# Loading and converting the first chunk of the masked weight by quarters, with fewer zero products ahead of it

## The chip, the cores and the metric

The kernel runs on one core of a Trainium2 chip. Its time is the device time of one execution in microseconds (us); the time before is the median of 3 runs, 395.11 us (395.07 to 395.71). A core has a tensor engine for matrix products (PE, with its weight loads shown apart as PEld), a vector engine (DVE), a scalar engine (ACT), a general engine (POOL) and a queue engine that mostly issues transfers (SP). Transfers (DMAs) run on 16 DMA engines beside them. Products are summed in PSUM, of which the kernel uses 8 banks; everything else lies in SBUF.

## The reference, cut to what matters

The input x has 8 batches of 256 tokens by 1024 features. Two residual layers follow each other. The first adds to x a dense layer and a difference whose weight is the sign that an integer mask stands for, scaled by a number per batch:

```python
def _L0_cond_ref(hidden_states, W, b, coeff, mask):
    output = jnp.einsum('bsi,oi->bso', hidden_states, W) + b
    sign = (2 * mask - 1).astype(hidden_states.dtype)
    diff = jnp.einsum('bsi,bio->bso', hidden_states, sign)
    return output + diff * coeff[:, None, None]

x = x + _L0_cond_ref(x, L0_cond_W, L0_cond_b, condB_coeff, mask)
x = x + _L1_cond_ref(x, itok, L1_cond_W, L1_cond_b, L1_cond_lora_As, L1_cond_lora_Bs)
```

The second adds a dense layer with weight W1, one bias, and a rank-16 adapter chosen per batch. All is in float32. The kernel folds the first layer into one weight per batch, W0 + coeff * (2 * mask - 1), plus the identity for the residual.

## The kernel before, in words

Batch 0 is computed directly and is what the change touches. Its weight is built in eight chunks `c` of 128 input features; each chunk has two parts `i` of 512 output columns. For each part, SP issues a load of 128 x 512 mask integers and a load of 128 x 512 numbers of W0 (256 KB each; the loop at the call of `first_loads`, recorded at L400). ACT converts the mask to float as 2 * coeff * mask - coeff (`convert`, L488), DVE adds W0 in place (`add`, recorded at L387), and PE multiplies each 128 x 128 block of the sum with the 128 x 256 block of x (L570). The last step has eight output blocks for each chunk, four for each part, accumulated in four banks. A float32 product appears in the trace as two MATMUL records.

Two small numbers per batch, `two_c` and `neg_c` (L445), hold 2 * coeff and -coeff on all partitions. They come from a tiny product of PE (L435) on the loaded coefficients, and the first conversion needs them. Before and behind this product PE multiplies zeros into a bank that nobody reads (`idle`, L422): 256 and 128 columns before it, 256, 256 and 128 columns behind it. The real products of batch 0 follow in PE's queue directly behind the last zeros.

`parts(c)` says in what pieces a chunk is converted and summed. In chunk 0 part 0 goes in two pieces of 256 columns, so that the first two output blocks can start once the first piece is there; part 1 and all other chunks go in pieces of 512 columns. The loads are never smaller than 512 columns.

After batch 0 come batches 1 to 3 by a seven-product scheme (`seven`, products at L761), then the second layer for four batches at once (`second_layer`, L1089, L1144, L1223, L1254), and then the same for batches 4 to 7. In batch 1 the weight is made in another way: ACT writes W0 - coeff (`shifted`, L500), and DVE adds 2 * coeff * mask to it (L645). DVE also makes the sums and differences of weights and tokens that the scheme needs, and adds the identity to W0 in SBUF, one 128 x 128 block per chunk (`identity`, L387).

The order of every engine's queue is fixed when the kernel is built, by a planner (`Plan`): each step has an estimated duration, PE's steps follow each other without a gap from a start that the code sets (`plan.pe = 5.2` for batch 0), and the other engines' steps are placed by the due times that follow from PE's. So a change of that start shifts due times and can swap steps on DVE, ACT, POOL and SP anywhere in the program.

In the second group of four, `left_again` loads again from DRAM the sums of the second layer's weights that the first group saved; for the name in `HALVES` two of them are loaded by two DMAs each, of 128 KB.

Of the kernel before, what the change touches and what calls it, by code (L numbers as in the profile page):

```python
# [9 lines left out]
I32 = mybir.dt.int32  # L10
# [3 lines left out]
P = 128  # L14
OH = 512
CG = 2
OQ = 256
# [6 lines left out]
A22_AT = 40.0  # L24
INNER_MOVED, INNER_AT = ({}, {o: ("t1", "t2", "t3", "t4") for o in ("S3", "A22")}), 24.0
SAVED = {(o, n) for o in ("A11", "S1", "S4") for n in ("a11", "s1")}
HALVES = ("A11",)
EARLIEST = 35.0
SHIFTED, MASKED = 5.2, 1.8
LEAF, SLACK = 30.0, 1.5  # L30
ALONE = 8.0
# [273 lines left out]
def kernel(  # L305
# [17 lines left out]
    NG, _, _, T = x0T.shape  # L323
# [41 lines left out]
    def small(name, a, b):  # L365
        return Buf(name, "S", (a, b))
# [12 lines left out]
    plan = Plan(2.9)  # L379
# [14 lines left out]
    def dma(engine, o, x, nbytes, due=None, ahead=None, slack=0.0):  # L394
        busy = {"SP": 0.37, "ACT": 0.36, "POOL": 0.53}[engine]
        reads = [x] if isinstance(x, Ref) else []
        writes = [o] if isinstance(o, Ref) else []

        def emit():
            ENGINE[engine].dma_start(  # L400
                o.ap() if isinstance(o, Ref) else o, x.ap() if isinstance(x, Ref) else x
            )

        return plan.task(
            engine, busy, plan.LATENCY[engine] + slack, emit, reads, writes, due, ahead, nbytes
        )

    def pe(n, busy, emit, reads, writes):
        return plan.task("PE", busy, 0.17, emit, reads, writes)
# [9 lines left out]
    def idle(*columns):  # L419
        def emit():  # L420
            for n in columns:
                nc.tensor.matmul(  # L422
                    idle_ps.t[:, 0, :n], lhsT=zeros[:, :P], rhs=zeros[:, :n], start=True, stop=True
                )

        pe(1, sum(columns) / 290, emit, (), (idle_ps((0,)),))
# [11 lines left out]
        (h_sb(h_rows), lb_pad((0, 1))),  # L438
        (c_ps((0,)),),
    )  # L440
    idle(T, T, T // 2)
    plan.pe = 5.2
    for o, f in ((two_c, 2.0), (neg_c, -1.0)):
        dve(
            lambda o=o, f=f: nc.vector.tensor_scalar_mul(o.t, c_ps.t[:, 0, :B], f),  # L445
# [6 lines left out]
    def x0_ref(p, c=None):  # L452
        return x0[p](ALL if c is None else (c,), (lambda t: t) if c is None else (lambda t: t[:, c]))
# [4 lines left out]
    def part(a, i):  # L458
        flat = a.rearrange("p i f -> (p i f)")
        return flat.rearrange("(i p f) -> i p f", i=2, p=P)[i]  # L460

    def parts(c):
        every = slice(0, OH)
        if c == 0:
            return [(0, slice(0, OQ)), (0, slice(OQ, OH)), (1, every)]
        return [(0, every), (1, every)]

    def halves(o):
        return tuple(q for q in range(2) if o.start < (q + 1) * OQ and o.stop > q * OQ)
# [38 lines left out]
    def w_part(c, i, o):  # L508
        return w_b0[c](tuple((i, q) for q in halves(o)), lambda t: t[:, i, o])

    def w0_part(c, i, o):
        return w0_sb(
            tuple((c, i, q) for q in halves(o)),
            lambda t: t[:, c, :].rearrange("p (h o) -> p h o", h=2)[:, i, o],
        )

    def first_loads(*load):
        k = dma(*load)
        k.rank = 1.0 + 0.001 * k.n

    every = slice(0, OH)
    for c in range(NC):
        for i in range(2):
            w = w_part(c, i, every)
            m = w.buf(w.keys, lambda t, f=w.index: f(t).bitcast(I32))
            first_loads("SP", m, part(mask[0, c], i), P * OH * 4)
            first_loads("SP", w0_part(c, i, every), part(w0T[c], i), P * OH * 4)
            if c < CG and i == 0:
                first_loads(("ACT", "SP")[c], x0_ref(0, c), part(x0T[0], c), P * T * 4)
            elif c % CG == 0 and i == 0:  # L530
                first_loads("SP", x0_ref(c // CG), x0T[c // CG], P * CG * T * 4)
# [19 lines left out]
    for c in range(NC):  # L551
        h, q = divmod(c * P, OH)
        for i, o in parts(c):
            w = w_part(c, i, o)
            m = w.buf(w.keys, lambda t, f=w.index: f(t).bitcast(I32))
            n = o.stop - o.start
            convert(w, m, 0, n)
            if c >= 1 and i == h and o.start <= q < o.stop:
                d = w_b0[c](((h, q // OQ),), lambda t, h=h, q=q: t[:, h, q : q + P])
                add(d, d, ident((0,)), P)  # L560
            add(w, w, w0_part(c, i, o), n)
    for c in range(NC):
        for i, o in parts(c):
            ots = [i * TPH + j for j in range(o.start // P, o.stop // P)]
            w = w_part(c, i, o)
# [297 lines left out]

    SOON = EARLIEST
    A_OF = {"a11": (0, 0), "a12": (0, 1), "a22": (1, 1)}
# [53 lines left out]
    def left_again(name, pairs=()):  # L919
# [21 lines left out]
        for n in saved:  # L941
            t = small(f"ls_{name}_{n}", 4, P)
            step = 2 if name in HALVES else 4
            for i in range(0, 4, step):
# [731 lines left out]
```

## Time and profile before

| what | value |
|---|---|
| median of 3 runs | 395.11 us |
| the profiled execution | 395.16 us |
| its span, first to last instruction | 393.5 us |
| PE busy in the span | 389.7 us (99%), 2920 records |
| DVE busy | 352.2 us (90%), 596 instructions |
| ACT busy | 169.8 us (43%), 314 instructions |
| DMA from the hardware queue of SP | 68.76 MB |
| zero products, ahead of and behind the tiny product | 10 records, from 0.90 to 5.46 us |
| products of batch 0 | 128 records, from 5.46 us, 29.03 us of the chain |

Columns of a timeline row: start in us from the span's start, length in us, engine, line, operation, output<-input tiles, shapes, number of instructions merged, and in brackets the idle time ahead of the row and what ended it. PE's records overlap, since matmuls are pipelined: the work rate is read from the distance between starts, not from a record's length. The profiled execution lasted 1.7 us longer than its span, and 0.05 us longer than the median.

### The profile page before, as it was taken

The page shows a single profiled execution, that of the slowest core. Times are in us where ns is not written, and L with a number is a line of the kernel's source. Part 1 is how long each engine was busy: PE and PEld are TensorE (multiplying, and loading weights), DVE is VectorE, ACT ScalarE, POOL GpSimd, SP SyncE. Part 2 cuts the span into 40 slices and gives each one's busy share as a digit, 9 for nine tenths or more (in the row PEclk, how much of TensorE's full clock was granted, in tenths as well). Part 3 has the DMA queues.
Part 4 walks back from the last instruction along what each step waited for, and adds up shares of the span by engine and source line. Part 5 has one row for each costly group of instructions (what it writes and reads, how often), then busy time and mean ns, then how long its engine had stood idle before and what let it go on. Part 6 is the DMA issues. An engine that isn't in the chain of part 4 may idle for free.

```text
span 393.5 us, 7725 instructions
## 1 busy us (share of the span) xinstructions
PE 389.7 (99%) x2920; PEld 363.8 (92%) x2920; DVE 352.2 (90%) x596; ACT 169.8 (43%) x314; POOL 84.2 (21%) x140
## 2 busy tenths in 40 slices
PE   9999999999999999999999999999999999999997
PEld 7889999999978898988899999999999789999896
DVE  3569999999897799989999989999996999999886
ACT  5469677516245221315615647373222563431210
POOL 1000202234734264252250330000000131241000
PEclk9999999999999999999999999999999999999999
DMA  8999999994899969989999998503702999995804
GB/s 290 389 389 410 404 300 389 318 346 156 198 269 290 270 239 368 417 247 317 348 347 338 291 260 304 191 1 108 242 0 61 262 238 265 324 255 101 263 31 185
DMA packets 39382, 102.50 MB, mean 261 GB/s; under 512 B 5170, under 2 KB 6322, under 8 KB 39346
## 3 DMA queue, kind: packets, MB, share of 16 engines
q1 hardware_dynamic: 27216, 68.76, 49.0%
q0 software_dynamic: 11840, 33.05, 32.5%
q8 instruction: 23, 0.38, 0.4%
q10 hardware_dynamic: 290, 0.20, 0.2%
q14 instruction: 13, 0.11, 0.1%
HBM read 65.82 MB, written 21.50 MB: 222 GB/s over the span
## 4 chain that ended last, share of the span: by engine, by line
PE 99%; DVE 0%; issue 0%
PE bank L761 44%; PE bank L1089 31%; PE bank L1144 11%; PE bank L570 7%; PE bank L1254 2%; PE bank L1223 2%; PE bank L422 1%; PE bank L1444 0%; PE bank L435 0%; DVE big L387 0%
## 5 line engine op out<-in xcount | busy, mean ns | idle before, releaser
L387 DVE TENSOR_TENSOR big<-big,big 128x1024 f32<-128x1024 f32 (+2 forms) x106 | 106.1, 1019 | 0.4 <-PE bank L761 0.4
L761 PE MATMUL bank<-small,big 128*128 128x128 f32 x896 | 104.6, 275 | 0.0
L761 PEld LDWEIGHTS bank<-small,big 128*128 128x128 f32 x896 | 102.3, 192 | 0.0
L387 DVE TENSOR_TENSOR big<-bank,big 128x512 f32<-128x512 f32 (+2 forms) x115 | 75.5, 678 | 15.0 <-PE bank L1089 8.2
L488 ACT ACTIVATE big<-big,neg_c,two_c 128x1024 f32<-128x1024 int32 (+2 forms) x65 | 71.1, 1123 | 19.4 <-DMA big<-mask 19.3
L761 PE MATMUL bank<-big,big 128*128 128x128 f32 x672 | 78.3, 275 | 0.0
L761 PEld LDWEIGHTS bank<-big,big 128*128 128x128 f32 x672 | 76.8, 192 | 0.1
L387 DVE TENSOR_TENSOR big<-big,w 128x1024 f32<-128x1024 f32 (+2 forms) x55 | 56.5, 1048 | 6.3 <-ACT big L488 3.4
L672 ACT ACTIVATE big<-bank,b 128x128 f32<-128x128 f32 x112 | 33.3, 367 | 52.7 <-PE bank L761 47.0
L391 ACT COPY bank<-bank 128x128 f32<-128x128 f32 (+1 forms) x42 | 14.4, 357 | 89.6 <-PE bank L1144 48.3
L1089 PE MATMUL bank<-small,small 128*128 128x256 f32 x168 | 40.2, 379 | 0.0
L1089 PEld LDWEIGHTS bank<-small,small 128*128 128x128 f32 x168 | 31.4, 190 | 3.9
L391 ACT COPY big<-bank 128x512 f32<-128x512 f32 x32 | 17.7, 594 | 36.0 <-PE bank L1254 17.4
L1089 PE MATMUL bank<-big,small 128*128 128x256 f32 x120 | 30.5, 381 | 0.0
L570 PE MATMUL bank<-small,big 128*128 128x256 f32 x128 | 29.2, 393 | 0.0
L570 PEld LDWEIGHTS bank<-small,big 128*128 128x128 f32 x128 | 25.4, 199 | 3.6
L477 POOL DMA_DIRECT2D big<-w x10 | 12.5, 1254 | 71.9 <-DMA big<-mask 56.5
L1089 PEld LDWEIGHTS bank<-big,small 128*128 128x128 f32 x120 | 21.4, 191 | 2.5 <-DVE big L387 0.4
L477 POOL DMA_DIRECT2D big<-big x14 | 12.3, 931 | 46.6 <-ACT big L991 36.1
L1089 PE MATMUL bank<-big,big 128*128 128x256 f32 x88 | 21.1, 383 | 0.0
L387 DVE TENSOR_TENSOR small<-big,small 128x512 f32<-128x512 f32 (+1 forms) x41 | 21.1, 522 | 0.0
L1089 PEld LDWEIGHTS bank<-big,big 128*128 128x128 f32 x88 | 16.5, 190 | 3.2 <-issue 0.4
(106 smaller groups left out, 468.6 us busy)
## 6 DMA issues: line engine op xcount, KB each, us to landing
big<-mask SPq DMA_DIRECT2D x56, 512.0 KB, 9.1
big<-xT SPq DMA_DIRECT2D x14, 512.0 KB, 8.6
big<-big POOLq DMA_DIRECT2D x14, 512.0 KB, 9.0
big<-w POOLq DMA_DIRECT2D x10, 512.0 KB, 10.3
big<-mask SPq DMA_DIRECT2D x16, 256.0 KB, 5.4
w<-w0T SPq DMA_DIRECT2D x16, 256.0 KB, 5.4
big<-w1T SPq DMA_DIRECT2D x8, 512.0 KB, 14.5
leaf_S_s<-small POOLq DMA_DIRECT2D x16, 256.0 KB, 7.6
```

Of the source, the lines that this page charges most:

```text
L387: return dve(lambda: f(o.ap(), x.ap(), y.ap()), n, (x, y), (o,), due, ahead)
L391: "ACT", n / 1200 + 0.06, 0.11, lambda: nc.scalar.copy(o.ap(), x.ap()), (x,), (o,), due
L422: nc.tensor.matmul(idle_ps.t[:, 0, :n], lhsT=zeros[:, :P], rhs=zeros[:, :n], start=True, stop=True)
L477: lambda: nc.gpsimd.dma_start(o.ap(), z.ap(), accum_op=ALU.add),
L488: lambda: nc.scalar.activation(o.ap(), x.ap(), AF.Identity, bias=neg_c.t[:, b : b + 1], scale=two_c.t[:, b : b + 1]),
L570: nc.tensor.matmul(dense[ot // 2].t[:, ot % 2, :], lhsT=w_b0[c].t[:, h, j * P : (j + 1) * P], rhs=x0[c // CG].t[:, c % CG, :], start=c == ...
L672: lambda o=o, p=p, bias=bias: nc.scalar.activation(o.ap(), p.ap(), AF.Identity, bias=bias.ap()),
L761: nc.tensor.matmul(ps[:, j, :], lhsT=l[:, c, j * P : (j + 1) * P], rhs=m[:, 2 * a + c, :], start=first and a == 0 and c == 0 and j == 0, s ...
L1089: nc.tensor.matmul(ps.t[:, j, :], lhsT=lt[:, c, j * P : (j + 1) * P], rhs=rt[:, c, :], start=start and c == 0 and j == 0, stop=False, skip ...
L1144: lambda: nc.tensor.matmul(o.ap(), lhsT=l.ap(), rhs=r.ap(), start=start, stop=False, skip_group_check=True),
L1223: nc.tensor.matmul(ph.t[i * S : i * S + R, 0, :], lhsT=la.t[:, i, c, :], rhs=y[GB * group + i, c // TPH].t[:, c % TPH, :], start=c == 0, s ...
L1254: nc.tensor.matmul(ps[b].t[:, j, :], lhsT=lb_pad.t[rows, o : o + P], rhs=h_sb.t[rows, :], start=j == 0, stop=j == 1, skip_group_check=True,)
```

## The change

- The load of part 0 of chunk 0 is issued as four DMAs of 128 x 256 (128 KB each: mask, W0, mask, W0) in place of two of 128 x 512. SP so has 4 issues where it had 2, and every later load is two places further back in its queue.
- Part 1 of chunk 0 is converted and summed in two pieces of 256 columns in place of one of 512. Its loads stay whole.
- Behind the tiny product PE multiplies 256 and 128 columns of zeros in place of 256, 256 and 128.
- The planner's start of batch 0's products is 4.75 in place of 5.2.
- `HALVES` is empty: in the second group the two saved sums of A11 are loaded by one DMA each (256 KB) in place of two (128 KB).

The order of PE's real products is unchanged. On the other engines the planner swaps some neighbours. The ones near the change: on DVE one addition of the identity to W0 (128 x 128) goes from ahead of the first three L645 steps of batch 1 to behind them; on ACT one L500 step of batch 1 goes ahead of the last conversion of batch 0. Later: on DVE a few sums of batches 1 to 3 and of the second layer swap places with a neighbour, on ACT some reads of banks swap with conversions, on POOL four stores of the second layer's sums change places, and on SP one mask load of the second group goes behind the loads of the saved sums.

```diff
-HALVES = ("A11",)
+HALVES = ()
+IDLE, FIRST = (256, 128), 4.75
+PARTS = 4
...
-    idle(T, T, T // 2)
-    plan.pe = 5.2
+    idle(*IDLE)
+    plan.pe = FIRST
...
     def parts(c):
         every = slice(0, OH)
         if c == 0:
-            return [(0, slice(0, OQ)), (0, slice(OQ, OH)), (1, every)]
+            first = [slice(0, OQ), slice(OQ, OH)]
+            return [(0, o) for o in first] + [(1, o) for o in (first if PARTS == 4 else [every])]
         return [(0, every), (1, every)]
...
     for c in range(NC):
         for i in range(2):
-            w = w_part(c, i, every)
-            m = w.buf(w.keys, lambda t, f=w.index: f(t).bitcast(I32))
-            first_loads("SP", m, part(mask[0, c], i), P * OH * 4)
-            first_loads("SP", w0_part(c, i, every), part(w0T[c], i), P * OH * 4)
+            for o in ((slice(0, OQ), slice(OQ, OH)) if c == i == 0 else (every,)):
+                n = P * (o.stop - o.start) * 4
+                wo = w_part(c, i, o)
+                m = wo.buf(wo.keys, lambda t, f=wo.index: f(t).bitcast(I32))
+                first_loads("SP", m, part(mask[0, c], i)[:, o], n)
+                first_loads("SP", w0_part(c, i, o), part(w0T[c], i)[:, o], n)
```

## The prediction

> **What bounds the kernel now.** I read the chain of waits first, then PE's timeline of the first microseconds, then the record lengths of batch 0's products, then the other engines around the first product, and last DVE's timeline, to see what an earlier PE would run into.
>
> ```profile
> PE 99%; DVE 0%; issue 0%
> PE bank L761 44%; PE bank L1089 31%; PE bank L1144 11%; PE bank L570 7%; PE bank L1254 2%; PE bank L1223 2%; PE bank L422 1%; PE bank L1444 0%; PE bank L435 0%; DVE big L387 0%
> ```
>
> The whole span is PE's queue from 0.90 us on. So only two things shorten it: fewer records on PE, or records that run faster. Anything else helps only if it ends a wait of PE, and PE has nearly none: the starts from 8.4 us on follow each other at 0.216 us (256 columns) or 0.112 us (128), and all that exceeds this, at changes of shape, is 2.1 us in 382.
>
> ```profile
> 0.90 1.62 PE L422 MATMUL bank<-const-float32-0.0 128*128 128x256 f32 x4 [0.90 <-PEq L1665]
> 2.45 0.79 PE L435 MATMUL bank<-lb,h 1*128 1x128 f32 x2
> 3.17 2.50 PE L422 MATMUL bank<-const-float32-0.0 128*128 128x256 f32 x6
> 5.46 3.77 PE L570 MATMUL bank<-small,big 128*128 128x256 f32 x10
> ```
>
> The six records of zeros fill 3.17 to 5.46 us; the change takes two of 256 columns out. How much time that is depends on the clock, which the lengths of batch 0's records show, up to 8.5 us and behind 8.6 us (count, then least, median and greatest length in ns):
>
> ```profile
> L570 PE MATMUL bank<-small,big x8: 381/634/635, 5.5 to 8.4; 128*128 128x256 f32 x8
> ```
> ```profile
> L570 PE MATMUL bank<-small,big x121: 379/379/381, 8.4 to 34.3; 128*128 128x256 f32 x121
> ```
>
> Until about 8.4 us a record lasts 634 ns and starts come 0.427 us apart; behind it 379 ns and 0.216 us. PE runs at half speed first, zeros included, and at full speed from 8.38 us to the end. So a microsecond gained before 8.38 us is worth only half a microsecond at the end, if the moment of the switch stays.
>
> ```profile
> 0.86 0.38 SPq L400 DMA_DIRECT2D big<-mask  x1
> ...
> 1.30 0.42 SPq L400 DMA_DIRECT2D w<-w0T  x1
> 1.42 0.36 ACTq L400 DMA_DIRECT2D small<-x0T  x1
> ...
> 3.36 0.15 DVE L445 TENSOR_SCALAR neg_c<-bank 128x8 f32<-128x8 f32 x1
> ...
> 3.75 1.09 ACT L488 ACTIVATE big<-big,neg_c,two_c 128x256 f32<-128x256 int32 x2 [0.44 <-DMA big<-mask]
> ...
> 4.76 0.76 DVE L387 TENSOR_TENSOR big<-big,w 128x256 f32<-128x256 f32 x2 [1.24 <-DMA w<-w0T]
> ```
>
> The first sum waits for the W0 load and ends at 5.18 us; PE reaches its first real product at 5.46 us, 0.28 us later. So taking zeros out alone would gain little: the sum has to come earlier too.
>
> **The zeros.** Six records begin at 3.17, 3.76, 4.19, 4.61, 5.04 and 5.25 us, the first with 0.16 us of start-up. Without two of 0.427 us they end at 4.61 us. If PE went straight on, two records of batch 0 would move into the half-speed time, which saves two full-speed records: 2 x 0.216 = 0.43 us. That is the most this part can give.
>
> **The first sum.** `neg_c` is done at 3.52 us; nothing of the change moves that. The mask's half load now carries 8 packets of 1 KB per DMA engine in place of 8 of 2 KB; near the start of the trace the former last 46 ns, the latter 84. The whole load lands at 3.66 us, the half about 8 x 38 = 0.3 us sooner, so ACT now waits for `neg_c`. It starts at about 3.59; the first conversion of 256 columns lasted 0.60: 4.19. The W0 half lands before that: today W0 ends at 4.63 behind 8 mask packets and beside x, and per engine 8 x 38 ns are saved in each of the two loads, 0.6 us: 4.03. x itself landed at 4.81; its 8 packets share the engines with lighter loads, so about 4.2. DVE starts 0.04 behind ACT (as at 6.25 behind 6.21) and lasts 0.43: 4.66. PE starts 0.07 later (the least such distance in the trace), at 4.73, and pays the start-up of 0.16 again, because it stood still from 4.61. Its second record then stands where a steady flow begun at 4.89 would have it, 0.57 us before today's 5.46. That is 0.57 / 0.427 = 1.34 records, worth 1.34 x 0.216 = **0.29 us** at the end. Bounds: 0.43 from above (no stop); from below, if the W0 half landed no sooner than today's whole, PE would start at 5.16 + 0.16 and gain 0.07.
>
> **Two more issues on SP.** An issue lasts 0.38 to 0.43 us, so each later load is issued 0.8 us later. The DMA engines don't run dry: the first packets ran 1.02 us behind their issue, so the load now fifth (issued near 2.7) can run from 3.7, while the four halves and x keep each engine busy with 40 packets of 46 ns from 2.47 to 4.31. What remains is the packets' price: 32 of 46 ns in place of 16 of 84 is +0.13 us for all loads behind, since the engines are full (near 390 GB/s) up to about 45 us. In batch 0 each sum ends 1.65 to 1.74 us before its product from the second part on: 0.13 later and 0.29 earlier leave 1.2. No stall.
>
> **Part 1 in quarters.** Two conversions cost 1.09 us (today's pair at 3.75) where one costs 0.81, two sums 0.76 where one costs 0.69. PE wants the first quarter at 4.89 + 8 x 0.427 = 8.3 us. The load lands near 5.5; conversion 0.6 and sum 0.43 make 6.6. Hidden by 1.6 us, and it buys nothing; uncovered, the whole would cost at most 0.35.
>
> **Swaps near the change.** The L500 step that goes ahead of the last conversion on ACT (1.13 us) delays it by up to 0.45; its sum ends at 30.07 and its product starts at 32.81, so 1.9 us stay. What counts is on DVE:
>
> ```profile
> 30.10 0.29 DVE L387 TENSOR_TENSOR w<-w,ident 128x128 f32<-128x128 f32 x1
> 30.31 1.28 DVE L645 SCALAR_TENSOR_TENSOR big<-big,two_c,big 128x1024 f32<-128x1024 int32 x1
> 31.51 0.69 DVE L746 TENSOR_TENSOR small<-big 128x512 f32<-128x512 f32 x1
> 32.86 2.57 DVE L645 SCALAR_TENSOR_TENSOR big<-big,two_c,big 128x1024 f32<-128x1024 int32 x2 [0.66 <-DMA big<-mask]
> ```
> ```profile
> 33.00:65.00 32.00, 32.00 (x281) 31.80 (x281) 31.97 (x31) 23.56 (x39) 4.75 (x4) 1.00 1.04 375
> ```
>
> The second line (window; sum; PE, PEld, DVE, ACT, POOL busy) shows DVE full: from the mask wait at 32.86 it stands still nowhere until 106 us. In that stretch all delays add. The addition of the identity at 30.10 takes 0.21 us of time in which DVE waits anyway; the change puts it behind 32.86, where it costs 0.21. With the load's 0.13 DVE is 0.34 us late. The tightest sum of the stretch is the second of the pair at 61.84, which ends at 64.20; its product starts at 64.91. PE wants it at 64.91 - 0.29 - 0.07 = 64.55, DVE has it at 64.20 + 0.34 = 64.54. That is even, and I take **0.05 us** as lost there (0 to 0.29). The next tightest have 1.03 us (45.3) and 1.38 us (81.0).
>
> **The rest.** Behind 106 us DVE waits for PE's banks again and again, so it moves with PE; the swaps there exchange neighbours of 0.7 to 1.2 us where no bank read goes later. The loads of `HALVES` are issued at 243.7 to 249.2 us, land within 4.8 us and serve products at 297.9: 45 us of cover; one mask load goes two issues back, 0.8 us. POOL's stores serve loads a hundred microseconds later. The tail behind PE's last record (390.3 to 393.5) keeps its steps. Price 0; if a cover failed, a step's length, 0.7 to 1.2.
>
> **The sum**: 395.16 - 0.29 + 0.05 = 394.92 against the profiled execution, which stands 0.05 above the median; so 394.9.
>
> **A rule of the Trainium skill beside this.** "TensorE: Matmul & The Clock Gate", Part 1: The HAM clock gate, says that PE starts at half clock and is released after a busy window of about 3.4 us, windows that run freely and don't start with the kernel. The trace agrees on half speed. By the page a stop inside the window that would have released the clock costs a whole window, and it speaks against a change that makes PE wait: by it, as an estimate, the switch comes 3.4 us later and the time is about 396.6; if the stop falls outside, it is 394.9 as above.
>
> **Rivals.**
> - *The clock comes later* (slower than before). The change makes PE stop at 4.61, where today it runs on. For: today PE ran without a stop from 3.17 to the switch at 8.38, 5.21 us; if that time counts from the last stop, the switch comes at 4.73 + 5.21 = 9.94, 1.56 us later, half of it lost: 394.9 + 0.78 = 395.7. If the 7.48 us from the first record (0.90) count anew from there, it comes at 12.2, and the time is 396.8. Against: the stop is 0.12 us, and the stops at 2.31 and 3.04 today did not keep the switch from coming. It is over 0.2% slower if the switch comes behind 10.4 us.
> - *The clock comes earlier*, with real products: 5.46 to 8.38 is 2.92 us; 4.73 + 2.92 = 7.65, 0.73 us of half speed less, 0.36 gained: 394.5. Against: zeros keep PE just as busy.
> - *DVE eats it.* The 64.9 us product waits the whole 0.29 or somewhat more: 395.1 to 395.3. It is slower by 0.2% only if DVE is 1.4 us late there, for which I find 0.34.
> - *The start doesn't move*: the W0 half or x lands as today, gain 0.07: 395.1.
>
> **How the numbers follow.** 0.2% is 0.8 us, about what a measurement of this kernel can tell from no change. Chances: forecast (394.7 to 395.0) 0.55; later clock 0.19, of which 0.13 past 0.2%; earlier clock 0.13, of which 0.09 past 0.2%, where it comes earlier still; DVE and the unmoved start 0.13. So faster 0.10, same 0.76, slower 0.14. The range, 394.3 to 396.0, runs from the earlier clock to between the two later ones; what it leaves out is about 0.2.
>
> **What would show it.** PE's zeros end at 4.6 us and the first L570 record starts at 4.7 to 4.9, behind a stop of about 0.1; the first conversion starts near 3.6, the first sum near 4.25. L570 records change from 634 to 379 ns at about 8.4 us; a change at 9.9 or 11.8 means the later clock. The first L761 record stands at 34.25 in place of 34.54. DVE has no gap from 33 to 106 us; a wait of PE on DVE near 64.6 is the second rival. I am wrong if the switch moves, or if PE waits anywhere behind 35 us for more than a few tenths.

## The result and the profile after

The changed kernel takes 396.39 us (median of 10 runs, 395.74 to 397.57) against 395.05 us of the kernel before (median of 10 runs beside it, 394.69 to 395.71). The ratio is 1.0036, with a 95% interval of 1.0025 to 1.0046: it is slower by 1.3 us. The prediction said 394.9, within 0.2% of before.

The profiled execution after the change took 396.84 us with a span of 395.2 us, 1.7 us more than the span before. Its page has this chain of waits (share of the span by engine, then by line; L766 is the former L761, L1094 the former L1089, L575 the former L570):

```profile
PE 82%; DMA 8%; DVE 6%; issue 2%; SPq 1%; DVEq 0%
PE bank L766 37%; PE bank L1094 30%; PE bank L1149 11%; DMA big<-mask 4%; DVE big L389 4%; DMA w<-w0T 3%; PE bank L1259 2%; PE bank L1228 2%; DVE big L650 2%; SPq L402 1%; PE bank L1449 0%; DVE small L751 0%; DVE w L389 0%; DVEq L650 0%
```

Before, 99% of the chain was PE's own queue. Now 15% of it are loads of masks and W0, SP's issues of them, and DVE's work on them. The end no longer goes back through PE to the start: it goes back through DVE and the first loads.

The timeline of the first microseconds shows what came as foreseen and what did not:

```profile
2.71 0.43 SPq L402 DMA_DIRECT2D big<-mask  x1
...
3.17 1.65 PE L424 MATMUL bank<-const-float32-0.0 128*128 128x256 f32 x4
...
3.56 0.60 ACT L491 ACTIVATE big<-big,neg_c,two_c 128x256 f32<-128x256 int32 x1 [0.26 <-DVE neg_c L447]
...
4.19 0.43 DVE L389 TENSOR_TENSOR big<-big,w 128x256 f32<-128x256 f32 x1 [0.67 <-ACT big L491]
4.57 0.60 ACT L491 ACTIVATE big<-big,neg_c,two_c 128x256 f32<-128x256 int32 x1 [0.41 <-DMA big<-mask]
...
4.67 5.15 PE L575 MATMUL bank<-small,big 128*128 128x256 f32 x15
...
5.56 0.42 DVE L389 TENSOR_TENSOR big<-big,w 128x256 f32<-128x256 f32 x1 [0.95 <-DMA w<-w0T]
...
6.76 1.09 ACT L491 ACTIVATE big<-big,neg_c,two_c 128x256 f32<-128x256 int32 x2 [1.59 <-DMA big<-mask]
```

The first conversion (3.56), the first sum (4.19) and the first product (4.67) stand where the prediction put them, the product 0.80 us sooner than before. But then the loads are late: the second W0 half holds the second sum until 5.56, and mask part 1, issued at 2.71 in place of 1.77, holds the conversion of part 1 until 6.76. By its last packet that mask landed at 6.73 us; before the change it landed at 5.38.

Here are the DMA engines in windows of 2 us (window; sum; PE, PEld, DVE, ACT, POOL busy with counts; PE clock; busy share of the DMA engines; GB/s). Before the change:

```profile
2.00:4.00 2.00, 2.00 (x7) 1.46 (x6) 0.24 (x2) 1.55 (x3) 0.31 (x1) 1.00 0.89 298
4.00:6.00 2.00, 2.00 (x7) 1.64 (x7) 0.96 (x3) 1.44 (x3) 0.00 (x0) 1.00 1.06 385
6.00:8.00 2.00, 2.00 (x6) 1.58 (x5) 1.01 (x3) 1.03 (x2) 0.00 (x0) 1.00 1.06 389
```

After it:

```profile
2.00:4.00 2.00, 2.00 (x7) 1.46 (x6) 0.24 (x2) 1.73 (x3) 0.31 (x1) 1.00 0.91 265
4.00:6.00 2.00, 2.00 (x6) 1.59 (x6) 0.86 (x3) 0.75 (x2) 0.00 (x0) 1.00 0.93 228
6.00:8.00 2.00, 2.00 (x6) 1.39 (x6) 0.69 (x3) 1.09 (x2) 0.00 (x0) 1.00 1.04 372
```

Between 4 and 6 us the engines count as busy 93% of the time but move 228 GB/s in place of 385. Their packets show where the time went: the usual one of 1 KB takes 46 ns and the usual one of 2 KB 84 ns, but between 3.5 and 5.5 us the slowest took 769 and 841 ns. (Such a stall is not the change's alone: a second execution of the kernel before moved 299 GB/s between 4 and 6 us, with packets of up to 694 ns, but the loads that it issued from 5 us on landed only 0.3 to 0.5 us behind those of the first.) The first 10 us of the two executions, before and after:

```profile
DMA packets 1774, 2.92 MB, mean 292 GB/s; under 512 B 221, under 2 KB 477, under 8 KB 1774
```
```profile
DMA packets 1821, 2.49 MB, mean 249 GB/s; under 512 B 223, under 2 KB 991, under 8 KB 1821
```

The 0.43 MB that are missing are 1.1 us at 390 GB/s. The stream is late from then on: the loads behind it land 1.3 to 2.0 us later, most of those that before were issued up to 19 us 1.6 us later, and those behind them 2.1 us later. What adds the last half microsecond was not looked for.

Where PE pays for it, in the waits of its weight loads between 35 and 70 us after the change (waiter <- what it waited for: us in total, times, longest):

```profile
PEld bank L766 <- DVE big L389: 0.7, 2, 0.5
PEld bank L766 <- DVE big L650: 0.6, 1, 0.6
```

And DVE, at the head of its unbroken stretch, which began at 32.86 us before:

```profile
34.92 2.64 DVE L650 SCALAR_TENSOR_TENSOR big<-big,two_c,big 128x1024 f32<-128x1024 int32 x2 [0.52 <-DMA big<-mask]
```

DVE is 2.06 us late there, and nothing behind it gives the time back. PE waits at 40.0, 46.0 and 66.2 us, 1.54 us in all with the start-up behind each stop. Another 0.67 us goes in batch 0 itself, where PE waits for late sums at 9.7 to 12.2 us.

**A sum that every profile obeys.** PE runs at half speed until its clock is released, which I take here as the first record that is followed after 0.216 us (8.42 us in the execution before, 8.15 after). All work behind it is fixed. So a later first product and a later release cost half of their shift, a stop ahead of the release costs half, and a wait behind it costs the whole. For the execution after the change: first product 0.80 earlier, -0.40; release 0.27 earlier, -0.14; start-up at the first product, 0.16, +0.08; waits behind the release, +2.23. Sum +1.77; PE's last record starts 1.72 us later. In the experiments this sum met the measured shift within 0.1 us in all 16 profiled executions other than the first of before. It is bookkeeping on PE's own timeline: it is used below to say where an execution lost its time, and does not say why.

With this way of reading it, the release comes too late when the clock was released while PE stood still. The trace's own record of the granted clock shows this in two executions, "split only" (9.08 us, not 10.12) and "both by ACT" (7.27, not 8.27); in the others that have such a record it lies within 0.2 us of the figure used here.

### The profile page after: what moved, and what is told of

The parts are those of the page before. It is cut to its first block, busy times and chain, and to the rows that moved or that the text cites. A ratio compares the mean times of both kernels' runs of the same rounds, so it can differ in the third digit from the quotient of the medians.

```text
span 395.2 us, 7723 instructions
## 1 busy us (share of the span) xinstructions
PE 390.5 (99%) x2918; PEld 363.1 (92%) x2918; DVE 351.8 (89%) x597; ACT 170.4 (43%) x315; POOL 84.2 (21%) x140
## 4 chain that ended last, share of the span: by engine, by line
PE 82%; DMA 8%; DVE 6%; issue 2%; SPq 1%; DVEq 0%
PE bank L766 37%; PE bank L1094 30%; PE bank L1149 11%; DMA big<-mask 4%; DVE big L389 4%; DMA w<-w0T 3%; PE bank L1259 2%; PE bank L1228 2%; DVE big L650 2%; SPq L402 1%; PE bank L1449 0%; DVE small L751 0%; DVE w L389 0%; DVEq L650 0%
## 5 line engine op out<-in xcount | busy, mean ns | idle before, releaser
L766 PE MATMUL bank<-small,big 128*128 128x128 f32 x896 | 105.2, 275 | 0.3 <-DVE big L389 0.3
L766 PEld LDWEIGHTS bank<-small,big 128*128 128x128 f32 x896 | 102.5, 192 | 0.7 <-DVE big L389 0.7
L766 PE MATMUL bank<-big,big 128*128 128x128 f32 x672 | 78.6, 275 | 0.4 <-DVE big L650 0.4
L766 PEld LDWEIGHTS bank<-big,big 128*128 128x128 f32 x672 | 76.9, 192 | 0.7 <-DVE big L650 0.6
L1094 PE MATMUL bank<-small,small 128*128 128x256 f32 x168 | 40.2, 379 | 0.0
L1094 PEld LDWEIGHTS bank<-small,small 128*128 128x128 f32 x168 | 31.4, 190 | 4.0
L1094 PE MATMUL bank<-big,small 128*128 128x256 f32 x120 | 30.5, 380 | 0.0
L575 PE MATMUL bank<-small,big 128*128 128x256 f32 x128 | 30.0, 397 | 0.2 <-DVE big L389 0.2
L575 PEld LDWEIGHTS bank<-small,big 128*128 128x128 f32 x128 | 25.1, 199 | 4.8 <-DVE big L389 1.2
L480 POOL DMA_DIRECT2D big<-w x10 | 12.4, 1254 | 74.0 <-DMA big<-mask 58.5
L1094 PEld LDWEIGHTS bank<-big,small 128*128 128x128 f32 x120 | 21.3, 191 | 2.5 <-DVE big L389 0.4
L1094 PE MATMUL bank<-big,big 128*128 128x256 f32 x88 | 21.1, 383 | 0.0
L1094 PEld LDWEIGHTS bank<-big,big 128*128 128x128 f32 x88 | 16.5, 190 | 3.2 <-issue 0.4
```

Of the source, the lines that this page charges most:

```text
L480: lambda: nc.gpsimd.dma_start(o.ap(), z.ap(), accum_op=ALU.add),
L575: nc.tensor.matmul(dense[ot // 2].t[:, ot % 2, :], lhsT=w_b0[c].t[:, h, j * P : (j + 1) * P], rhs=x0[c // CG].t[:, c % CG, :], start=c == ...
L766: nc.tensor.matmul(ps[:, j, :], lhsT=l[:, c, j * P : (j + 1) * P], rhs=m[:, 2 * a + c, :], start=first and a == 0 and c == 0 and j == 0, s ...
L1094: nc.tensor.matmul(ps.t[:, j, :], lhsT=lt[:, c, j * P : (j + 1) * P], rhs=rt[:, c, :], start=start and c == 0 and j == 0, stop=False, skip ...
```

## Experiments

Three theories; the quoted expectations call the first two A and B, and their C is that the tiny load on POOL collides with the small loads. **The small loads**: four loads of 128 KB at the head of SP's queue make the whole stream late, whether by their issues or by their packets. **The rest of the change**: part 1 in quarters, the swaps of the planner on DVE and the stop at the start cost the time. **The clock**: it is released later, since PE stops at 4.6 us (the first rival).

**Whole first loads.** All of the change but the split of the loads.

```diff
-            for o in ((slice(0, OQ), slice(OQ, OH)) if c == i == 0 else (every,)):
+            for o in (every,):
```

> The changed kernel with the first part of mask and W0 loaded whole again (two loads of 256 KB); fewer zeros, quarter sums and the planner's swaps behind 36 us stay. Theory A (the four small loads leave the DMA engines without work near 4 to 5 us, the whole stream of loads comes 1.3 to 1.6 us late, and this uses up the lead of the sums over the products): the mask of part 1 lands near 5.4 us, no product waits behind 35 us, PE stands still about 0.5 us before its first real product, time 394.7 to 395.2. Theory B (the swapped steps on DVE and ACT make PE wait near 40, 46 and 66 us): these waits stay, 395.9 to 396.4. Theory C (the tiny load on POOL collides with the small loads): as A.

Measured: 395.62 us (394.88 to 397.25, 11 runs), ratio 1.0012 (1.0001 to 1.0023). In its profile, mask part 1 lands at 5.54 us, 2.91 MB are there by 10 us, and DVE's stretch begins at 32.84. PE stops for 0.46 us ahead of the first product and waits 0.57 us at 44.2 and 64.0. Without the split two thirds of the loss are gone. The single runs spread more than those of before, and the profiled execution (394.88) is the fastest of them, with an early release at 6.78.

**Only the split.** The kernel before with the four small loads and nothing else.

```diff
+            for o in ((slice(0, OQ), slice(OQ, OH)) if c == i == 0 else (every,)):
...
-                first_loads("SP", m, part(mask[0, c], i), P * OH * 4)
+                first_loads("SP", m, part(mask[0, c], i)[:, o], n)
```

> The kernel before with only the four small loads. Theory A: the mask of part 1 lands near 6.7 us in place of 5.4, DVE begins its unbroken stretch 1.6 us late and PE waits near 65 us and perhaps before, 0.8 to 1.3 us in all, time 395.9 to 396.4. Theory B: no waits, 395.0 to 395.3. Theory C: as A.

Measured: 396.98 us (396.76 to 397.24, 5 runs), ratio 1.0044 (1.0030 to 1.0058). Mask part 1 lands at 8.19 us. The split alone costs as much as the whole change. PE's weight loads wait for the sum of part 1 in this kernel:

```profile
PEld bank L572 <- DVE big L387: 1.4, 1, 1.4
```

The terms, as in the table below: stop of 0.92 from 8.88 taken as ahead of the release, +0.46; release at 10.12, +0.85; waits behind it, +0.21. But the clock came within this stop, as the first record behind it shows:

```profile
L572 PE MATMUL bank<-small,big x1: 483/483/483, 9.8 to 9.8; 128*128 128x256 f32 x1
```

A first record behind a stop lasts 483 ns at full speed and 793 to 796 at half speed. With the granted clock's 9.08 us (8.38 in the first execution of before), the clock costs 0.35, the stop 0.10 ahead of it and 0.72 behind it, the start-up 0.10 and the waits 0.21: 1.48, as measured. So most of this loss is the wait for part 1. The start of the products has not moved here, so the product of part 1 is wanted only at 8.9 us, and still it has to wait.

**The 32 bytes of itok.** POOL loads them at 1.62 us; here SP does so later, so that nothing of POOL's queue meets the small loads.

```diff
-    dma("POOL", itok_sb((0,)), itok, 32, due=50.0, ahead=20.0)
+    dma("SP", itok_sb((0,)), itok, 32, due=50.0, ahead=12.0)
```

> The changed kernel with the 32-byte load of the adapter numbers taken from POOL's queue at the start and issued by SP near 25 us. Theory C: the DMA engines keep working between 4 and 5.3 us, the mask of part 1 lands at 5.8 us or sooner, the waits behind 35 us go, time 394.9 to 395.3. Theory A: the mask of part 1 still lands near 6.7, time 396.0 to 396.6. Theory B: 396.0 to 396.6.

Measured: 396.51 us (396.40 to 397.20, 6 runs), ratio 1.0035 (1.0023 to 1.0047); mask part 1 lands at 7.26. No help: that load is not what the packets meet.

**One small load issued by ACT.** The second mask half goes out behind x on ACT's queue. Nothing else is moved.

```diff
-                first_loads("SP", m, part(mask[0, c], i)[:, o], n)
+                first_loads("SP", m, part(mask[0, c], i)[:, o], n, by="ACT" if c == i == 0 and o.start else None)
```

> The changed kernel with one of the four small loads, the second half of the mask, issued by ACT behind x, so that SP issues all later loads one place (0.47 us) sooner; everything else as in the changed kernel. Theory A, with SP's issues as what starves the engines: the mask of part 1 lands 0.4 to 0.6 us sooner (near 6.2), and the waits shrink by as much, time 395.6 to 396.1. If the number and size of the loads starve them and not the issue: landing and time as changed, 396.2 to 396.6. The first conversion starts up to 0.3 us later than in the changed kernel, which costs up to 0.15 us.

Measured: 395.72 us (395.37 to 396.46, 11 runs), ratio 1.0017 (1.0008 to 1.0026). Half of the loss is back, and by 10 us 2.63 MB have come. But mask part 1 still lands at 7.42: 13 of its 16 pieces were there by 5.85, and the last came 1.6 us behind these.

**Issues against packets.** Both of the next two are the kernel with whole loads, in which the order of all other work is the same. One issues each of the two first loads as two of 64 rows (four issues, 2 KB packets):

```diff
+                for r in range(0, P, rows):
+                    ENGINE[engine].dma_start(to[r : r + rows], of[r : r + rows])
```

> The kernel with whole first loads, but each of the two is issued as two DMAs of 64 rows by 512 columns: four issues on SP as after the change, and packets of 2 KB as before it. If the later issues make the stream late, mask part 1 is issued at 2.7 us and lands at 6.7 us as after the change (with whole loads 5.54), PE waits a few tenths near 8, 40 and 46 us, and the time is 396.1 to 396.8. If the small packets do it, mask part 1 lands at 5.4 to 5.8 us and the time is that of whole loads, 395.2 to 395.8.

The other keeps two issues, but each gathers two pieces of 256 columns per row, so that packets are of 1 KB:

```diff
-                first_loads("SP", m, part(mask[0, c], i)[:, o], n)
+                first_loads("SP", doubled(m), spread(mask[0, c]), n)
```

> The kernel with whole first loads, two issues as before the change, but each of the two DMAs gathers two pieces of 256 columns per row, so that its packets are of 1 KB. (The second piece comes from other columns of the mask and of W0, so batch 0 and what follows from its weight are computed from other numbers.) If the later issues make the stream late, mask part 1 lands at 5.4 to 5.8 us and the time is 395.2 to 395.8. If the small packets do it, mask part 1 lands at 6.5 us or later, with PE waits behind 35 us, and the time is 396.1 to 396.8.

Measured: 396.81 us for four issues (396.43 to 397.20, 5 runs), ratio 1.0042 (1.0029 to 1.0055); 396.55 us for small packets (395.89 to 397.62, 7 runs), ratio 1.0040 (1.0026 to 1.0055). Each alone costs as much as the change, so neither expectation as an either-or held. Mask part 1 landed at 6.35 and at 6.55. With four issues it was issued only at 3.37 us, not at 2.7, since the issues of 64 rows follow each other after 0.62 us. The profile of the second, in 0.25 us slices of its first 10 us (busy tenths of the DMA engines, GB/s, totals), has the same hole behind 4 us:

```profile
DMA  0000000057999999679668899999999999999999
GB/s 0 0 0 0 0 0 0 17 61 188 332 328 348 373 307 299 135 98 246 193 246 262 328 410 402 393 393 393 418 393 377 406 402 397 393 393 402 385 393 393
DMA packets 1869, 2.63 MB, mean 263 GB/s; under 512 B 203, under 2 KB 971, under 8 KB 1869
```

The waits behind 35 us that the expectation named for small packets did not come: the first product was at 6.1 us in both, since the first sum had to wait for its W0, so PE was late itself. The terms there: +0.32 for the start, +0.63 for a release at 9.69, nothing behind it. So small packets cost as much as the change, but in another place: at the first product and at the release, and not behind 35 us.

**Whole loads without the stop.** The 256 columns of zeros are back, so PE runs on to the first product at 5.46.

```diff
-    idle(*IDLE)
+    idle(*IDLE, extra=(T,))
```

> The kernel with whole first loads, and the 256 columns of zeros put back, the order of all other work as after the change. PE then runs on until 5.46 us without the stop of 0.56 us. If the rest of the change (part 1 in quarters, the swaps of the planner, the whole loads of the second group) is free, as the prediction had it, and the stop is what held whole loads at 395.62, the time is that of before, 394.8 to 395.3, with a narrower spread. If the swaps cost, it stays at 395.6 and PE waits behind 35 us.

Measured: 395.66 us (394.93 to 396.11, 11 runs) beside 395.18 of before (24 runs), ratio 1.0009 (0.9999 to 1.0018). So the stop (0.46 us in the profile, not 0.56) is not what held whole loads at 395.62. What the rest of the change costs is at most 0.7 us by this interval, and can't be told from nothing. In this profile one of the 16 pieces of W0 part 1 fell 0.7 us behind at 6 us (15 by 6.15, the last at 6.86) although no load was small.

**Both second halves issued by ACT.** SP then has two issues ahead of part 1, as before, and there are still four small loads. Beside the line above it has the same for W0:

```diff
-                first_loads("SP", w0_part(c, i, o), part(w0T[c], i)[:, o], n)
+                first_loads("SP", w0_part(c, i, o), part(w0T[c], i)[:, o], n, by="ACT" if c == i == 0 and o.start else None)
```

> As after the change, but both second halves (mask and W0, 128 KB each) are issued by ACT behind x, so SP has two issues ahead of part 1 as before the change, and the small loads are still four. The first conversion gets about 0.35 us later, since ACT issues twice more ahead of it, so the first product comes at about 5.0 us. If the later issues on SP make the stream late, mask part 1, issued at 1.77 us, lands at 5.4 to 5.8 us, no PE wait is seen behind 35 us and the time is 394.8 to 395.3. If the small packets or the number of loads do it, mask part 1 lands at 6.7 us or later and the time is 395.7 or more.

Measured: 397.29 us (395.28 to 398.61, 12 runs), ratio 1.0048 (1.0030 to 1.0065). The runs lie in two groups, five up to 396.06 and seven from 397.27 on, and the profiled execution (395.39) is in the lower. The stream came as the issue side of the expectation has it: mask part 1 at 5.48 us, 2.70 MB by 10 us, no wait behind 35 us. The time did not follow, because PE stopped twice in batch 0: 0.66 us ahead of the first product, whose conversion ACT began only at 4.17, and 0.82 us from 7.13 for the second W0 half, which ACT issued at 2.28 and which landed at 7.38.

**Second looks.** Executions of one kernel differ, so the decisive kernels were profiled again: the kernel before, the two that set issues against packets, the changed kernel three more times, and the last one, to see what its two groups are.

> The kernel before, unchanged, in a second profiled execution. If the late load stream belongs to the small loads, mask part 1 lands near 5.4 us and DVE's unbroken stretch begins at 32.6 to 33.3 us, as in the first. If the stream is late by chance, either may be 1 to 2 us later. If the moment at which the clock is released varies between executions of one kernel, it is not 8.4 us here but anywhere from 6.6 to 10.1; if it follows from the kernel, it is 8.2 to 8.6.

> The changed kernel in a second profiled execution. If the late stream belongs to the small loads, mask part 1 lands at 6.4 us or later and DVE's unbroken stretch begins at 34.2 to 35.2 us; if it is chance, it may begin near 33. Clock release: 7.9 to 8.4 us if it follows from the kernel, anywhere from 6.6 to 10.1 if it varies. The time less that of before is half of the shift of the first product, of the release and of the stops ahead of it, and the whole of PE's later waits.

> Four issues with packets of 2 KB, a second profiled execution. If the issues' share in the late stream is systematic, DVE's unbroken stretch begins at 33.9 to 34.7 us (34.28 in the first); if it was chance, it may begin near 33.

> Two issues with packets of 1 KB, a second profiled execution (the second half of part 0 is read from other columns, so batch 0 is computed from other numbers). If the small packets' share is systematic, mask part 1 lands at 6.2 to 6.9 us and DVE's unbroken stretch begins at 33.3 to 33.8 us (33.52 in the first); if it was chance, mask part 1 may land near 5.4.

> The changed kernel in a third profiled execution. If the late loads carry the loss, PE's waits behind the release sum to 0.6 us or more, as in the first two (2.2 and 0.6 us), and mask part 1 lands at 6.4 us or later. If the later clock carries it, the release is at 9.5 us or later and PE's waits behind it are under 0.4 us. Either way the terms must sum to the time lost within 0.1 us.

> The changed kernel in a fourth profiled execution, with the same two readings: waits of 0.6 us or more behind the release for the late loads, a release at 9.5 us or later for the clock.

> Both second halves issued by ACT, a second profiled execution. The timed runs stood in two groups, 395.3 to 396.1 us and 397.3 to 398.6 us, and the first profile lay in the lower. If the clock makes the groups, an execution of the upper group shows a release 3 us or more behind the 8.3 us of the first, and one of the lower group a release near 8.3. If late loads make them, the release stays near 8.3 in the upper group too, and PE waits 1.5 us or more elsewhere.

Measured, one run each: the kernel before 395.27 us, the changed kernel 396.61, 396.46 and 396.09, four issues 397.76, small packets 397.41, both halves by ACT 397.61; runs of the kernel before beside them took 395.43 and 394.67. All in one table; "MB" is what had come by 10 us, "DVE" the start of its unbroken stretch, and the last five columns are the terms of the sum in us against the first execution of before, and PE's measured shift.

| execution | mask part 1 lands | MB | DVE | release | first product | release | stops | waits | measured |
|---|---|---|---|---|---|---|---|---|---|
| before | 5.38 | 2.92 | 32.86 | 8.42 | | | | | |
| before, second | 6.00 | 2.81 | 33.23 | 8.79 | 0 | +0.18 | 0 | 0 | +0.15 |
| after | 6.73 | 2.49 | 34.92 | 8.15 | -0.40 | -0.14 | +0.08 | +2.23 | +1.72 |
| after, second | 6.71 | 2.23 | 34.66 | 10.11 | -0.04 | +0.84 | +0.08 | +0.64 | +1.45 |
| after, third | 7.30 | 2.35 | 34.53 | 6.60 | -0.30 | -0.91 | +0.08 | +2.53 | +1.34 |
| after, fourth | 7.27 | 2.34 | 34.14 | 9.13 | -0.30 | +0.36 | +0.21 | +0.66 | +0.93 |
| whole loads | 5.54 | 2.91 | 32.84 | 6.78 | -0.20 | -0.82 | +0.08 | +0.57 | -0.44 |
| whole, no stop | 5.33 | 2.79 | 33.25 | 6.59 | 0 | -0.91 | 0 | +0.92 | -0.04 |
| split only | 8.19 | 2.27 | 34.76 | 10.12 | 0 | +0.85 | +0.46 | +0.21 | +1.48 |
| four issues | 6.35 | 2.27 | 34.28 | 9.57 | +0.34 | +0.57 | +0.08 | +0.50 | +1.41 |
| four issues, second | 8.47 | 1.97 | 35.92 | 12.43 | +0.39 | +2.00 | +0.08 | 0 | +2.52 |
| small packets | 6.55 | 2.63 | 33.52 | 9.69 | +0.32 | +0.63 | +0.08 | 0 | +1.06 |
| small packets, second | 7.49 | 2.48 | 33.53 | 12.11 | +0.32 | +1.84 | +0.08 | 0 | +2.17 |
| both by ACT | 5.48 | 2.70 | 33.30 | 8.27 | -0.10 | -0.08 | +0.49 | 0 | +0.28 |
| both by ACT, second | 5.41 | 2.73 | 33.58 | 12.42 | -0.10 | +2.00 | +0.62 | 0 | +2.49 |

The four executions of the changed kernel settle which of the two causes carries its loss. On average the waits behind the release cost 1.52 us, the stops ahead of it 0.11, the release costs 0.04, and the earlier first product gives 0.26 back: sum 1.41, against 1.36 measured. **The late stream carries it; the clock takes from one execution and gives to the next.** Two limits to this: four releases as scattered as these (6.60 to 10.11) leave the clock's mean share uncertain by about 0.4 us (estimate: half of their standard error, 0.75 us), and a wait is not the stream's alone where the clock came early. "Whole, no stop", whose loads came in time, waited 0.92 us with its release at 6.59, and the third execution, with 6.60, waited 2.53; so perhaps 0.9 of these, 0.2 of the mean, is PE's own lead. By place, about 0.5 of the mean is waited in batch 0 and 0.9 behind 35 us. Clock and waits are tied: where the clock is released late (second and fourth), PE itself is late, and so waits less for DVE. The third, with the earliest release, has the most waits. The lines of its weight loads, from the start to 70 us:

```profile
PEld bank L575 <- DVE big L389: 1.7, 2, 1.3
...
PEld bank L766 <- DVE big L389: 0.7, 2, 0.5
```

The first of these lines holds 1.06 us in which PE stood still for part 1 of chunk 0.

The stream itself is not chance: mask part 1 landed at 5.3 to 6.0 us in the four executions with whole loads, and at 6.4 to 8.5 in all eleven in which SP had three or four issues ahead of it, or two of 256 KB in packets of 1 KB (nine of the table, the one with itok moved and the one with one half on ACT). With both halves on ACT it came at 5.4 and 5.5.

The column "DVE" says more on issues against packets. Its stretch begins when a mask load of batch 1 lands, thirty microseconds behind the first loads. With two SP issues ahead of part 1 it begins at 32.84 to 33.25 us with packets of 2 KB, and at 33.30 to 33.58 with those of 1 KB (small packets and both by ACT, two executions each). With three issues (one half on ACT) it is 33.81, and with four 34.14 to 35.92 in eight executions, the one with itok moved among them (34.62), whatever the size of the packets. Small packets, both by ACT, one half on ACT, four issues, first executions:

```profile
33.52 2.56 DVE L659 SCALAR_TENSOR_TENSOR big<-big,two_c,big 128x1024 f32<-128x1024 int32 x2 [0.67 <-DMA big<-mask]
```
```profile
33.30 2.64 DVE L653 SCALAR_TENSOR_TENSOR big<-big,two_c,big 128x1024 f32<-128x1024 int32 x2 [0.53 <-DMA big<-mask]
```
```profile
33.81 2.63 DVE L653 SCALAR_TENSOR_TENSOR big<-big,two_c,big 128x1024 f32<-128x1024 int32 x2 [0.52 <-DMA big<-mask]
```
```profile
34.28 2.58 DVE L654 SCALAR_TENSOR_TENSOR big<-big,two_c,big 128x1024 f32<-128x1024 int32 x2 [0.63 <-DMA big<-mask]
```

So it is the two more issues on SP that make the stream late where DVE needs it; small packets alone make it 0.7 us late at most. "Both by ACT" shows what follows: with the same four small loads and nearly the release of the first execution after (8.27 and 8.15 as read here), PE waits nowhere behind 35 us, where that one waits 1.54 us, though PE is also 0.1 us later by then.

The two groups of the last kernel are the clock, as far as one execution of each can show. Batch 0's products, first execution (count, then least, median and greatest length in ns, first and last start), up to the release as read here, 8.27, and behind it:

```profile
L578 PE MATMUL bank<-small,big x5: 483/634/796, 5.3 to 7.9; 128*128 128x256 f32 x5
```
```profile
L578 PE MATMUL bank<-small,big x124: 379/379/483, 7.9 to 34.6; 128*128 128x256 f32 x124
```

And the second:

```profile
L578 PE MATMUL bank<-small,big x14: 521/634/794, 5.3 to 12.1; 128*128 128x256 f32 x14
```
```profile
L578 PE MATMUL bank<-small,big x106: 379/379/521, 12.1 to 34.9; 128*128 128x256 f32 x106
```

Both have the same first product and nearly the same stops (0.98 and 1.25 us with the start-ups). In the first the fifth record, behind the stop from 7.13, lasts 483 ns and so runs at full speed: 4 records run at half speed in one and 14, the last of them in part, in the other. Between the releases as read here lie 4.15 us, which is 2.07 us of time; with the stops' 0.13 it is the 2.2 us by which the two executions differ.

No version beat the kernel before: the best, with whole loads, stands at 1.0009 to 1.0012.

**What stays open** is why packets stall in the first 8 us, and so why two more issues, which delay part 1's issue by 0.94 us, make the stream up to 2.1 us late in the first execution after. Packets stall with four issues, with small packets and two issues, and at times with whole loads as well. The runs show which edit makes the stream late, not the mechanism behind the stalls.

## Why the prediction was wrong, point by point

- **"What bounds the kernel now"** was right for the kernel before, and it named its own weak spot: DVE without a gap from 33 to 106 us, 0.71 us of slack at 64.9. What was not drawn from it is that this makes the load stream a bound at one remove. A late stream moves DVE's start, and PE meets it a little later.
- **"The zeros"** and **"The first sum"** were right in the first execution after: zeros end at 4.61 (predicted 4.61), the first sum starts at 4.19 (4.23), the first product at 4.67 (4.73), with the start-up of 0.16 paid again. The gain of 0.29 was there, 0.32 by the terms (-0.40 + 0.08). In the second execution the first W0 half came at 4.79 and the product at 5.38, so the gain was near zero: the rival "the start doesn't move", in one execution out of four.
- **"Two more issues on SP"** is the step that failed, and its sentence is "The DMA engines don't run dry". It counted 40 packets of 46 ns per engine as if each engine would work them off without a pause, took the landing of the whole stream as a matter of packets, and got +0.13 us. Measured: the loads of the third chunk land 1.6 us later in the first execution (1.4 to 1.6 in the four), and 0.4 to 0.7 MB are missing by 10 us against 2.92. The other half of the step, that issues 0.8 us later stay hidden, failed too: with the two issues taken off SP, and the small packets kept, DVE's stretch begins at 33.30 and 33.58 us, with them at 34.14 to 34.92. The trace of before held a warning that I passed over: in it too the slowest packets of 2 KB between 2.0 and 3.5 us took 606 ns, and a sum from the usual packet leaves these out.
- **"Hidden by 1.6 us"** for part 1 failed with it: its first sum began at 7.50 us and so ended at about 7.9 in place of 6.6. PE wanted it at 8.1, so it just held here; in the third execution after PE stood still 1.06 us for it, and in the kernel with only the split 0.92.
- **"No stall" in batch 0** failed: 1.2 us were to be left, and PE waited at 9.7 to 12.2 us for 0.67 us.
- **The slack on DVE** was right as a mechanism and mis-sized by its input: DVE was to be 0.34 us late at 64.9 and was 2.06 late at the head of its stretch. By the prediction's own slack, 0.71 less the 0.07 from a sum to its product, 2.06 + 0.21 for the identity - 0.64 makes PE 1.63 us late there; the trace has PE 1.62 late behind the wait at 66.2. The rival "DVE eats it" (third in the list, called the second in the prediction's last paragraph) said 1.4 us of lateness would make the kernel slower by 0.2%, and found no source for it. The source was the step above.
- **"The clock comes later"**: the moment was taken as a property of the kernel, to be moved by the change. It is spread over microseconds within one kernel (6.60 to 10.11 in four executions after). On average it carried nothing of the loss here, within about 0.4 us. Where PE stops for long ahead of it, it may: of the six executions with a first product behind 6.1 us or a stop from 7.1 us, five had it at 9.6 to 12.4, and one at 8.27 (7.27 by the granted clock). That this rival's 395.7 and 396.8, and the estimate of 396.6 that the prediction made by the page, enclose or near the measured 396.39 is luck: they have the switch 1.6 to 3.8 us later, and on average of the four executions it came at 8.50.
- **"The rest", price 0**: not refuted, bounded at 0.7 us by the run with whole loads and no stop.

Two pages of the Trainium skill beside this. "TensorE: Matmul & The Clock Gate", Part 1: The HAM clock gate, has windows of 3.4 us that run freely and a release that varies by half a microsecond between runs. Free windows fit what is seen, a moment that moves from run to run of one kernel; half a microsecond does not: the earliest and the latest of four executions lie 3.5 us apart, about one such window, and two of the kernel with both halves on ACT 4.15 us. The page asks for sustained activity over a window and does not say how long a stop it bears; that one of 0.12 us costs a whole window was the prediction's reading of it, and these four executions don't show it. "DMA: Bandwidth & Descriptors", section Bandwidth, gives 138 GB/s for a transfer of 64 KB and 341 for one of 1 MB, measured on loads that the general engine issues (here SP and ACT issue them), and asks for large ones; the section Rules for kernel authors adds that two transfers to halves of the partitions aren't worth it. The first speaks against this change, the second against the experiment with 64 rows, and the runs agree in sign: with four loads of 128 KB the first 10 us brought 2.23 to 2.49 MB in place of 2.81 to 2.92, and with the loads of 64 rows the kernel was slower by 0.42%.

## What to carry to other kernels

Where an engine behind the bottleneck works without a gap on what a stream of loads brings, the stream's lateness passes through it to the bottleneck, tens of microseconds later: price a change at the head of a queue by when the last load of the stream lands, count the issues that it puts ahead of the stream, and don't price a landing by the usual packet alone. A start that gets half a microsecond earlier at half clock is worth a quarter at the end, so it must not cost a stream anything. And where a small effect is explained from one profile, take more of the same kernel first: here the same loss was made up of different parts in each of four.

## What the runs showed of the hardware that was not expected

- The release of PE's clock came anywhere between 6.59 and 12.43 us in the 15 executions of the table, 5.7 to 11.5 us behind PE's first record at 0.90. Each microsecond of it is half a microsecond of the kernel's time, as long as PE waits for nothing else: more than the whole change was thought to bring.
- While the DMA engines counted as 93% busy they moved 228 GB/s; packets that usually take 46 or 84 ns took up to 841 ns between 3.5 and 5.5 us, and in the fourth execution after up to 1740. Busy share of a DMA engine is not throughput.
- One of the 16 pieces of a load can come 0.9 us behind the other fifteen (with both halves on ACT, second execution: 15 pieces of W0 part 1 by 6.40 us, the last at 7.32), and what needs the load waits for the last: with one half on ACT, 15 pieces of mask part 1 were there by 6.60, the last at 7.42, and its conversion began at 7.45. It also happened with whole loads and no stop: 15 pieces of W0 part 1 by 6.15, the last at 6.86. There the last piece of the next load lagged too (6.83 and 7.95), as if one DMA engine had fallen behind; the trace does not name the engine.
- With two, three and four issues on SP ahead of part 1, the mask load at the head of DVE's unbroken stretch, thirty microseconds later, came at 32.84 to 33.58, 33.81, and 34.14 to 35.92 us.
